# Layer 2 of a graph network: the input added by VectorE, a norm's statistics from sums on ScalarE, 28 single places for the diagonals

## The chip, the cores and the metric

The kernel runs on one core of one Trainium2 chip. The metric is the device time of one execution in microseconds. Instructions are told apart by engine: PE (TensorE's matmuls; PEld is its loading of weights), DVE (VectorE), ACT (ScalarE), POOL (GpSimd) and SP (SyncE). Each has its own queue and works it off in order; semaphores tie the queues together. POOL issues the indirect transfers and SP the plain ones, and both kinds share 16 DMA engines.

## The reference

A graph network of two attention layers over 10,000 nodes and 170,000 given edges, all in float32. Cut to what matters:

```python
def gat_conv(x, src, dst, W, a_src, a_dst, bias):     # self loops are added to the edges
    xl = x @ W                                        # per head
    e = leaky_relu((xl @ a_src)[src] + (xl @ a_dst)[dst], 0.2)
    alpha = softmax of e over the edges of one dst
    return segment_sum(xl[src] * alpha, dst) + bias

h1 = relu(layer_norm(gat_conv(x, W1 ...), g1, be1)) + (x @ Wr1 + br1)     # 4 heads x 256
h2 = layer_norm(gat_conv(h1, W2 ...), g2, be2) + (h1 @ Wr2 + br2)         # 1 head, 768
out = plain_layer_norm(x + h2)          # mean and variance over 768, no weights
```

The change lies in the last two lines: the weighted sum over a node's neighbours, its norm, the two additions and the plain norm behind them.

## The kernel before

**Tiles and slots.** The nodes are sorted by their number of edges into 79 tiles of 128, one node to a partition. A tile `t` has `SLOTS[t]` slots: slot k holds, for each of its 128 nodes, the row of the node's k-th neighbour in the table `h1 @ W2`, 768 numbers and 2 attention terms (394 KB a slot). There are 1371 slots in layer 2, 17.4 a tile on average; the list `turns` lets large and small tiles alternate, 25 and 12 slots at the start, 18 and 17 at the end. Layer 2 starts at about 3185 us.

**The ring.** A `Ring` of `RING2 = 41` slots in SBUF holds the rows. The first slot of a tile is the nodes' own rows, a plain transfer by SP (L501); the other 1292 are indirect gathers by POOL (L472). Slot q + 41 is fetched into the place of slot q behind the last use of slot q, in the order of the program, so POOL waits until PE and DVE have both read it.

**A tile's work.** `weights_of(t)` makes the softmax weights `e`: small DVE operations and an exponential on ACT (L543). The weighted sum is shared by columns. DVE multiplies and adds columns 0 to 511 of one slot after another into `acc` (L573). For columns 512 to 767, `summed` lets ACT make a diagonal matrix of each slot's weights (L1298: the identity, scaled by `e`), and PE multiplies it with the slot's 256 columns (L1299) into the second part of the PSUM tile `rs[t]`. The bias `b2` goes into that sum by the identity, too (`add_b2`, L1308). `residual(t)` fills the first part of `rs[t]`: x by the identity (L1350), and `h1 @ Wr2` in 8 blocks for each of two column ranges, 512 and 256 wide (L1353). Each float32 matmul shows as two records in the profile. The operands hT and xt of `residual` are loaded by SP (L1257, L1258) two tiles ahead, into pieces of the memory in which layer 1 kept `w2` (the name `w` in the profile, `w_88` in the listings, means such pieces: hT, xt and the sums `h`); the first two tiles' are loaded earlier, into `firsts`.

**The norms.** `norms(t)` runs during the loop over the slots of tile t + 1, in steps at its start and at slots k = 3, 6 and 9 (`LEAD = 3`): the statistics of the weighted sum (L584, L586 on DVE; the standard deviation by logarithm and exponential on ACT, L588 and L589); then the scaling (L598, L600), the addition of `rs[t]` (L1363) and the statistics of the second norm (L584, L586, L588, L589 again); then `less` on DVE (L1367) and the output on ACT (L1369); then the output's indirect scatter on POOL (L1371).

**What sets the order.** Each engine's order is that in which the program is written. The loop over tile t writes `residual(t + 1)` first, then its slots; at slot `turn` of it the logits of tile t + 1, at `turn + 3` the softmax's rest, `add_b2`, the diagonals and PE's products of tile t + 1. So PE's order is `residual(t + 1)`, products of t + 1, `residual(t + 2)`, and so on, and on ACT the diagonals of tile t + 1 stand ahead of the norm of tile t. The diagonals have 5 places for groups of `G = 4`: 20 diagonals.

Of the kernel before, what the change touches and what calls it, by code (L numbers as in the profile page):

```python
# [28 lines left out]
F32 = mybir.dt.float32  # L29
I32 = mybir.dt.int32  # L30
BF16 = mybir.dt.bfloat16
AF = mybir.ActivationFunctionType
OP = mybir.AluOpType
AX = mybir.AxisListType

P = 128
# [12 lines left out]
G = 4  # L49
RING1 = 31  # L50
RING2 = 41
LEAD = 3
DIAGONALS = 5
ON_PE2 = 512
SHARE = 4
ON_PE1 = 5
# [30 lines left out]
def gnn_kernel(ctx, tc, x, x_cols, src, dst, src_col, dst_col, W1, a_src1, a_dst1, b1, g1, be1, Wr1, br1,  # L87
               W2, a_src2, a_dst2, b2, g2, be2, Wr2, br2, out, n_edges):
    nc = tc.nc
    N, D0 = out.shape  # L90
    H1, DH1 = a_src1.shape
    H2, DH2 = a_src2.shape
    C1, C2 = H1 * DH1, H2 * DH2
# [3 lines left out]
    NT = -(-N // P)  # L97
# [19 lines left out]
    x_d = dram.tile([NT, P, D0], F32, name="x_d")  # L117
# [458 lines left out]
    def pieces(a, width):  # L576

        return [a[:, c:c + width] for c in range(0, a.shape[1], width)]

    def deviation(small, parts):  # L580

        st = small.tile([P, len(parts), 6], F32, name="st")
        for j, a in enumerate(parts):
            nc.vector.bn_stats(st[:, j, :], a)  # L584
        mv = small.tile([P, 2], F32, name="mv")
        nc.vector.bn_aggr(mv, st.rearrange("p k s -> p (k s)"))  # L586
        sd = small.tile([P, 1], F32, name="sd")
        nc.scalar.activation(sd, mv[:, 1:2], AF.Ln, bias=eps)  # L588
        nc.scalar.activation(sd, sd, AF.Exp, scale=-0.5)  # L589
        return mv[:, 0:1], sd  # L590
# [254 lines left out]
    def begin_layer2(mem):  # L845


        rest = mem.shape[1]

        def at_end(n):  # L850
            nonlocal rest
            rest -= n
            return mem[:, rest:rest + n]

        firsts = [(at_end(C1), at_end(D0)) for _ in range(min(2, NT))]
        for t, (hT, xt) in enumerate(firsts):
            nc.sync.dma_start(hT, h1_d[turns[t]])
            nc.sync.dma_start(xt, x_d[turns[t]])
        wr2 = wr1.rearrange("p k n -> p (k n)")[:, :K1 * C2].rearrange("p (k n) -> p k n", n=C2)
        load(wr2, Wr2)  # L860
        br, ones = at_end(C2), at_end(P)
        yield
        nc.vector.memset(ones, 1.0)
        nc.vector.tensor_scalar(br, wr2[:, 0, :], br1_c[:, 0:1], None, op0=OP.mult)
        for k in range(1, K1):
            nc.vector.scalar_tensor_tensor(br, wr2[:, k, :], br1_c[:, k:k + 1], br, op0=OP.mult, op1=OP.add)
        yield wr2, firsts, br, ones, rest
# [367 lines left out]
    def ordered_layer2(mem, begun):  # L1235
# [4 lines left out]
        with tc.tile_pool(name="b2", bufs=1) as pool, tc.tile_pool(name="small2", bufs=2) as small, \  # L1240
# [2 lines left out]

            wr2, firsts, br, sums_of, rest = begun
            parts = pieces(w2.rearrange("p k n -> p (k n)")[:, :6 * C1], C1)
            held = mem.shape[1] // R2
            tail = pool.tile([P, RING2 - held, R2], F32, name="ring")
            views = [mem[:, :held * R2].rearrange("p (k n) -> p k n", n=R2), tail]
            ring = Ring(table2, RING2, dict(zip(FIRST, (TURNS[t] for t in turns))), views, at)

            def fetch_x(t):

                if t < 2:
                    hT, xt = firsts[t]
                else:
                    hT, xt = parts[t % 2], parts[2 + t % 2][:, :D0]
                    nc.sync.dma_start(hT, h1_d[turns[t]])  # L1257
                    nc.sync.dma_start(xt, x_d[turns[t]])  # L1258
                return hT.rearrange("p (k n) -> p k n", n=P), xt

            ins = {0: fetch_x(0)}
            ring.fetch(SLOTS[0])
            adds = [spread(pool, shift, "out", nc.sync)]
            b2_b = spread(pool, b2, "b2", nc.sync)
            ins[1] = fetch_x(1)
            g2_b, be2_b = (spread_to(to[:, :C2], v, nc.sync) for to, v in zip(norm_b, (g2, be2)))
            nc.vector.tensor_add(b2_b, b2_b, adds[0][:, :C2])
            adds.append(spread(pool, br2, "out", nc.sync))
# [17 lines left out]
            def weights_of(t):  # L1286
# [6 lines left out]

                def summed(e, lo, hi, more=None, m=0):
                    for k in range(lo, hi):
                        if (k - lo) % G == 0:
                            diagonals = pool.tile([P, G, P], F32, name="diagonals", bufs=DIAGONALS)
                        nc.scalar.activation(diagonals[:, (k - lo) % G, :], ident, AF.Copy, scale=e[:, k - lo, :])  # L1298
                        nc.tensor.matmul(to, diagonals[:, (k - lo) % G, :], ring.slot(at + k)[:, ON_PE2:C2],  # L1299
                                         start=False, stop=(k == n - 1), skip_group_check=True)  # L1300
                        if k - lo < m:
                            nc.tensor.matmul(more, diagonals[:, (k - lo) % G, :], ring.slot(at + k)[:, :ON_PE2],
                                             start=False, stop=(k - lo == m - 1), skip_group_check=True)
                        if k - lo == m - 1:
                            nc.scalar.copy(ring.slot(at + lo)[:, :ON_PE2], more)
# [37 lines left out]
            def residual(t):  # L1343


                hT, xt = ins.pop(t)
                r = ps_big.tile([P, 2 * BANK], F32, name="big")
                for c in range(0, C2, BANK):
                    d = min(C2, c + BANK)
                    nc.tensor.matmul(r[:, c:d], ident, xt[:, c:d], start=True, stop=False,  # L1350
                                     skip_group_check=True)
                    for j in range(K1):
                        nc.tensor.matmul(r[:, c:d], hT[:, j, :], wr2[:, j, c:d], start=False,  # L1353
                                         stop=(j == K1 - 1 and d < C2),
                                         skip_group_check=True)
                return r

            def norms(t, h, r, means):

                stats = deviation(small, [a for m in means for a in pieces(m, C2 - ON_PE2)])  # L1360
                yield
                scaled(h, means, stats, g2_b, be2_b)
                nc.vector.tensor_add(h, h, r[:, :C2])  # L1363
                mean, inv = deviation(small, pieces(h, C2 // 2))
                yield
                less = small.tile([P, 1], F32, name="less")
                nc.vector.scalar_tensor_tensor(less, mean, -1.0, inv, op0=OP.mult, op1=OP.mult)  # L1367
                o = pool.tile([P, C2], F32, name="out")
                nc.scalar.activation(o, h, AF.Identity, bias=less, scale=inv)  # L1369
                yield  # L1370
                nc.gpsimd.indirect_dma_start(  # L1371
                    out=out, out_offset=bass.IndirectOffsetOnAxis(ap=nodes(turns[t]), axis=0),
                    in_=o, in_offset=None, bounds_check=N - 1, oob_is_err=False)
# [10 lines left out]
            for t in range(NT):  # L1384
# [19 lines left out]
                for k in range(n):  # L1404
# [15 lines left out]
                        if not lo or k - lo >= whole(t):  # L1420
                            weigh(acc, row, weights[:, k - lo], ON_PE2, None if k else b2_b)
                    ring.fetch(FIRST[t] + k + 1 + ring.size)
                    if t + 2 < NT and k == n // 2:
                        ins[t + 2] = fetch_x(t + 2)
                ready += itertools.islice(ahead, 2 - len(ready))
                for _ in last:
                    pass
# [1 line left out]
                    nc.vector.tensor_add(be2_b, be2_b, adds[1])  # L1429
                    nc.vector.tensor_add(be2_b, be2_b, q[:, :C2])  # L1430
                last = norms(t, h, rs[t], [acc, rs[t][:, C2:2 * C2 - ON_PE2]])
                if t + 2 < NT and t + 2 not in ins:
                    ins[t + 2] = fetch_x(t + 2)
            for _ in last:
                pass

# [270 lines left out]
```

## Time and profile before

| | |
|---|---|
| median of 3 runs | 5286.99 us (5283.68 to 5294.54) |
| the profiled execution | 5287.85 us, span 5286.1 us, mean granted TensorE clock 0.943 |
| PE busy | 4742.8 us (90%), 14012 records |
| DVE busy | 4326.7 us (82%) |
| POOL busy | 3432.3 us (65%) |
| ACT busy | 3084.4 us (58%) |
| moved by DMA | 1588 MB, mean 300 GB/s |

The shares are means over the whole span. Layer 2 is the last 2.1 ms of it and has a mix of its own, so it is read by windows that lie within it. In rows of groups, what stands before the bar is the busy time and the mean time of one instruction in ns; behind it is the idle time of the engine just before such instructions, with what ended most of it. "issue" there is time in which the engine waited for nothing that the profile shows. In rows of a timeline, the first number is the start, the second the duration, and the bracket holds the idle time before it and what ended it.

### The profile page before, as it was taken

The page shows a single profiled execution, that of the slowest core. Times are in us where ns is not written, and L with a number is a line of the kernel's source. Part 1 is how long each engine was busy: PE and PEld are TensorE (multiplying, and loading weights), DVE is VectorE, ACT ScalarE, POOL GpSimd, SP SyncE. Part 2 cuts the span into 40 slices and gives each one's busy share as a digit, 9 for nine tenths or more (in the row PEclk, how much of TensorE's full clock was granted, in tenths as well). Part 3 has the DMA queues.
Part 4 walks back from the last instruction along what each step waited for, and adds up shares of the span by engine and source line. Part 5 has one row for each costly group of instructions (what it writes and reads, how often), then busy time and mean ns, then how long its engine had stood idle before and what let it go on. Part 6 is the DMA issues. An engine that isn't in the chain of part 4 may idle for free. (4 is left out here: it accounts for less than half of the span.)

```text
span 5286.1 us, 57927 instructions
## 1 busy us (share of the span) xinstructions
PE 4742.8 (90%) x14012; PEld 2650.4 (50%) x14012; DVE 4326.7 (82%) x7168; ACT 3084.4 (58%) x8710; POOL 3432.3 (65%) x3722
## 2 busy tenths in 40 slices
PE   9999998999999979899999997888888887888886
PEld 4444444554444434444445554555555555555554
DVE  7887877998998988889999975877878777777776
ACT  5744446899999988898999862322222322222222
POOL 6867756666777766677766626666666666666664
PEclk9999998999999989999999998889898898888888
DMA  4423459999999989999999959988899898888885
GB/s 153 131 94 129 112 174 338 350 365 367 382 387 395 376 299 339 344 372 380 376 373 370 349 199 328 327 316 313 313 320 315 310 320 305 305 299 301 303 302 191
DMA packets 433439, 1588.37 MB, mean 300 GB/s; under 512 B 77207, under 2 KB 82135, under 8 KB 433094
## 3 DMA queue, kind: packets, MB, share of 16 engines
q0 software_dynamic: 321040, 1283.72, 67.4%
q1 hardware_dynamic: 99490, 269.38, 14.1%
q10 hardware_dynamic: 12564, 31.47, 1.8%
q8 instruction: 118, 1.93, 0.1%
q14 instruction: 227, 1.86, 0.1%
HBM read 1426.26 MB, written 177.29 MB: 303 GB/s over the span
## 5 line engine op out<-in xcount | busy, mean ns | idle before, releaser
L472 POOL DMA_INDIRECT ring<-table,slots x2663 | 2636.4, 990 | 1490.6 <-issue 569.8
L562 ACT ACTIVATE ring<-ring,e 128x256 f32<-128x256 f32 x4468 | 1823.6, 502 | 65.7 <-DVE e L981 34.3
L573 DVE SCALAR_TENSOR_TENSOR acc<-ring,e,acc 128x512 f32<-128x512 f32 (+1 forms) x2280 | 1454.0, 638 | 104.2 <-PE acc L936 27.1
L569 DVE TENSOR_TENSOR acc<-acc,ring 128x1024 f32<-128x1024 f32 x869 | 1070.2, 1231 | 80.7 <-ACT ring L562 16.9
L1353 PE MATMUL big<-wr,w 128*128 128x512 f32 (+1 forms) x2464 | 877.3, 501 | 148.9 <-issue 147.4
L1299 PE MATMUL big<-ring,diagonals 128*128 128x256 f32 x2742 | 723.9, 419 | 182.6 <-issue 166.2
L1161 PE MATMUL half<-w,hT 128*128 128x512 f32 (+1 forms) x2528 | 844.0, 486 | 5.5 <-issue 5.2
L179 PE MATMUL big<-wr,xT 128*128 128x512 f32 x1896 | 836.4, 598 | 0.3 <-ACT xT L897 0.3
L1299 PEld LDWEIGHTS big<-ring,diagonals 128*128 128x128 f32 x2742 | 582.4, 213 | 323.4 <-issue 220.1
L1298 ACT ACTIVATE diagonals<-ident,e 128x128 f32<-128x128 f32 x1371 | 419.6, 388 | 546.9 <-PE big L1299 215.8
L1353 PEld LDWEIGHTS big<-wr,w 128*128 128x128 f32 x2464 | 480.6, 196 | 511.8 <-issue 482.7
L1161 PEld LDWEIGHTS half<-w,hT 128*128 128x128 f32 x2528 | 472.6, 189 | 349.7 <-issue 310.4
L179 PEld LDWEIGHTS big<-wr,xT 128*128 128x128 f32 x1896 | 358.0, 192 | 422.3 <-issue 421.6
L936 PE MATMUL acc<-ring,ident 128*128 128x512 f32 x992 | 469.5, 622 | 76.6 <-ACT ring L562 49.3
L588 ACT ACTIVATE sd<-mv,eps 128x1 f32<-128x1 f32 x237 | 69.3, 292 | 683.7 <-issue 261.1
L936 PEld LDWEIGHTS acc<-ring,ident 128*128 128x128 f32 x992 | 191.3, 198 | 317.0 <-issue 193.2
L694 ACT ACTIVATE scr<-scr 128x256 f32<-128x256 f32 x624 | 250.5, 403 | 160.7 <-DVE scr L687 155.6
L634 PE MATMUL one<-wr,mixed 128*128 128x512 f32 x702 | 307.6, 592 | 0.0
L699 POOL TENSOR_TENSOR row<-row,none 128x1024 f32<-128x1024 f32 x69 | 168.1, 2437 | 117.2 <-DVE scr L687 45.8
L634 PE MATMUL one<-w,xT 128*128 128x512 f32 x492 | 228.6, 602 | 7.7 <-DMA w<-in_W_dram 5.4
L584 DVE BATCH_NORM_STATS2 st<-big 128x6 f32<-128x256 f32 x79 | 33.4, 423 | 242.3 <-remote 122.8
L634 PEld LDWEIGHTS one<-wr,mixed 128*128 128x128 f32 x702 | 133.4, 190 | 167.9 <-issue 167.2
(239 smaller groups left out, 4334.0 us busy)
## 6 DMA issues: line engine op xcount, KB each, us to landing
ring<-table,slots POOLq DMA_INDIRECT x2663
h_d<-hT SPq DMA_DIRECT2D x79, 512.0 KB
table<-row SPq DMA_DIRECT2D x78, 516.0 KB
w<-h_d SPq DMA_DIRECT2D x77, 512.0 KB
table<-row SPq DMA_DIRECT2D x79, 385.0 KB
ring<-table SPq DMA_DIRECT2D x79, 385.0 KB
x_d<-xt SPq DMA_DIRECT2D x77, 384.0 KB
w<-x_d SPq DMA_DIRECT2D x77, 384.0 KB
```

What stands on the lines that cost most here:

```text
L179: nc.tensor.matmul(p[:, c:e], aT[:, j, :], w[:, j, c:e], start=(j == 0), stop=(j == k - 1))
L472: nc.gpsimd.indirect_dma_start(out=to, out_offset=None, in_=table, in_offset=bass.IndirectOffsetOnAxis(ap=index, axis=0), **more)
L562: nc.scalar.activation(row[:, s], row[:, s], AF.Copy, scale=e[:, h:h + 1])
L569: nc.vector.tensor_add(acc[:, :c], acc[:, :c], row[:, :c])
L573: nc.vector.scalar_tensor_tensor(acc[:, s], row[:, s], e[:, h:h + 1], (acc if first is None else first)[:, s], op0=OP.mult, op1=OP.add)
L634: nc.tensor.matmul(p, aT[:, j, :], w[:, j, :], start=(start and j == 0), stop=(j == k - 1), skip_group_check=True)
L694: nc.scalar.activation(m[:, s], m[:, s], AF.Copy, accum_out=row[:, C1 + i * H1 + h:C1 + i * H1 + h + 1])
L936: nc.tensor.matmul(acc[:, c:c + BANK], ident, ring.slot(q + k)[:, c:c + BANK], start=(k == 0), stop=(k == m - 1))
L1161: nc.tensor.matmul(q, hT[:, j, :], w2[:, j, c:c + q.shape[1]], start=(j == 0), stop=(j == K1 - 1))
L1298: nc.scalar.activation(diagonals[:, (k - lo) % G, :], ident, AF.Copy, scale=e[:, k - lo, :])
L1299: nc.tensor.matmul(to, diagonals[:, (k - lo) % G, :], ring.slot(at + k)[:, ON_PE2:C2], start=False, stop=(k == n - 1), skip_group_check=True)
L1353: nc.tensor.matmul(r[:, c:d], hT[:, j, :], wr2[:, j, c:d], start=False, stop=(j == K1 - 1 and d < C2), skip_group_check=True)
```

## The change

1. **x.** PE's product of the identity and x (L1350) goes. VectorE adds x to `h` in `norms(t)`, behind the addition of `rs[t]`. The loads are parted: `fetch_h` still loads hT two tiles ahead, `fetch_x` loads x one tile ahead, at the same point of the loop, into the same two pieces of `w`. That load now waits for VectorE's addition of the tile before the last, where it had waited for PE's reading.
2. **The second norm.** VectorE's statistics of it and `less` go. ScalarE makes them in two passes over the 768 columns that also sum up: a copy for the sum, then, with the negative mean as bias, a square for the variance; then logarithm, exponential and a product for the output's scale and bias.
3. **The diagonals.** 28 single places take the place of 5 groups of 4, 20 in a tile of their own and 8 in the ends of pieces of `w` that are 1024 columns long and hold 768. They are taken in turn.

```diff
-DIAGONALS = 5
+DIAGONALS = 20
...
+            diagonals = pieces(pool.tile([P, DIAGONALS * P], F32, name="diagonals"), P)
+            for part in parts[2:]:
+                diagonals += pieces(part[:, C1 - 2 * P:], P)
+            turning = itertools.cycle(diagonals)
...
+            def fetch_h(t):
+                if t < 2:
+                    hT = firsts[t]
+                else:
+                    hT = parts[t % 2]
+                    nc.sync.dma_start(hT, h1_d[turns[t]])
+                return hT.rearrange("p (k n) -> p k n", n=P)
             def fetch_x(t):
-                if t < 2:
-                    hT, xt = firsts[t]
-                else:
-                    hT, xt = parts[t % 2], parts[2 + t % 2][:, :D0]
-                    nc.sync.dma_start(hT, h1_d[turns[t]])
-                    nc.sync.dma_start(xt, x_d[turns[t]])
-                return hT.rearrange("p (k n) -> p k n", n=P), xt
+                xt = parts[2 + t % 2][:, :D0]
+                nc.sync.dma_start(xt, x_d[turns[t]])
+                return xt
...
                 def summed(e, lo, hi, more=None, m=0):
                     for k in range(lo, hi):
-                        if (k - lo) % G == 0:
-                            diagonals = pool.tile([P, G, P], F32, name="diagonals", bufs=DIAGONALS)
-                        nc.scalar.activation(diagonals[:, (k - lo) % G, :], ident, AF.Copy, scale=e[:, k - lo, :])
+                        diagonal = next(turning)
+                        nc.scalar.activation(diagonal, ident, AF.Copy, scale=e[:, k - lo, :])
...
             def residual(t):
-                hT, xt = ins.pop(t)
+                hT = ins.pop(t)
...
-                    nc.tensor.matmul(r[:, c:d], ident, xt[:, c:d], start=True, stop=False,
-                                     skip_group_check=True)
...
                 nc.vector.tensor_add(h, h, r[:, :C2])
-                mean, inv = deviation(small, pieces(h, C2 // 2))
+                nc.vector.tensor_add(h, h, xs.pop(t))
                 yield
-                less = small.tile([P, 1], F32, name="less")
-                nc.vector.scalar_tensor_tensor(less, mean, -1.0, inv, op0=OP.mult, op1=OP.mult)
                 o = pool.tile([P, C2], F32, name="out")
+                less, inv = (small.tile([P, 1], F32, name=n) for n in ("less", "inv"))
+                nc.scalar.activation(o, h, AF.Copy, accum_out=less)
+                nc.scalar.activation(less, less, AF.Copy, scale=-1.0 / C2)
+                nc.scalar.activation(o, h, AF.Square, bias=less, accum_out=inv)
+                nc.scalar.activation(inv, inv, AF.Ln, scale=1.0 / C2, bias=eps)
+                nc.scalar.activation(inv, inv, AF.Exp, scale=-0.5)
+                nc.scalar.activation(less, less, AF.Copy, scale=inv)
                 nc.scalar.activation(o, h, AF.Identity, bias=less, scale=inv)
...
-                    if t + 2 < NT and k == n // 2:
-                        ins[t + 2] = fetch_x(t + 2)
+                    if k == n // 2:
+                        if t + 2 < NT:
+                            ins[t + 2] = fetch_h(t + 2)
+                        if t + 1 < NT:
+                            xs[t + 1] = fetch_x(t + 1)
```

In the listings of the two programs, PE's queue where one tile's products end and the next tile's residual begins, before (`big` is `rs[t]`, `w_88` here xt in L1350's rows and hT in L1353's, `wr_89` Wr2, the semaphores in brackets are what a row waits for):

```order
L1299 MATMUL big<-ring,diagonals 128x256 [waits DMASW7_49,Activation_49]
L1350 MATMUL big<-w_88,ident 128x512 [waits DMAHW5_49,DVE_49,PE_49]
L1353 MATMUL big<-wr_89,w_88 128x512 [waits DMAHW4_49]
L1353 MATMUL big<-wr_89,w_88 128x512 x7
L1350 MATMUL big<-w_88,ident 128x256
L1353 MATMUL big<-wr_89,w_88 128x256 x8
L1308 MATMUL big<-b_22697,ident 128x256
L1299 MATMUL big<-ring,diagonals 128x256 [waits DMAHW2_49,Activation_49]
```

The same place after:

```order
L1306 MATMUL big<-ring,diagonals 128x256 [waits DMASW3_49,Activation_49]
L1358 MATMUL big<-wr_89,w_88 128x512 [waits DMAHW7_49,DVE_49,PE_49]
L1358 MATMUL big<-wr_89,w_88 128x512 x7
L1358 MATMUL big<-wr_89,w_88 128x256 x8
L1315 MATMUL big<-b_22696,ident 128x256
L1306 MATMUL big<-ring,diagonals 128x256 [waits DMAHW6_49,Activation_49]
```

Two matmuls are gone from each tile, and with them the wait for x's transfer; the rest stands as it did.

ACT's queue at a tile of 24 slots, before: the end of its diagonals, then the first norm's standard deviation of the tile before it (L588, L589, the first pair), the second norm's (the second pair), the output, and the exponential of the next tile:

```order
L1298 ACTIVATE diagonals<-ident,e 128x128 [waits PE_49]
L1298 ACTIVATE diagonals<-ident,e 128x128 x3
L588 ACTIVATE sd<-mv,eps 128x1 [waits DVE_49]
L589 ACTIVATE sd<-sd 128x1 [waits Activation_49]
L588 ACTIVATE sd<-mv,eps 128x1 [waits DVE_49]
L589 ACTIVATE sd<-sd 128x1 [waits Activation_49]
L1369 ACTIVATE out<-w_88,less,sd 128x768 [waits DMASW0_49,DVE_49]
L543 ACTIVATE e<-e 128x13 [waits DVE_49]
```

The same place after (`inv` is first the sum of squares, then the scale; `less` first the sum, then the bias):

```order
L1305 ACTIVATE diagonals<-ident,e 128x128 [waits PE_49] x16
L1305 ACTIVATE w_88<-ident,e 128x128 [waits PE_49] x7
L588 ACTIVATE sd<-mv,eps 128x1 [waits DVE_49]
L589 ACTIVATE sd<-sd 128x1 [waits Activation_49]
L1373 ACTIVATE out,less<-w_88 128x768 [waits DMASW0_49,DVE_49]
L1374 ACTIVATE less<-less 128x1 [waits Activation_49]
L1375 ACTIVATE out,inv<-w_88,less 128x768 [waits Activation_49]
L1376 ACTIVATE inv<-inv,eps 128x1 [waits Activation_49]
L1377 ACTIVATE inv<-inv 128x1 [waits Activation_49]
L1378 ACTIVATE less<-less,inv 128x1 [waits Activation_49]
L1379 ACTIVATE out<-w_88,less,inv 128x768 [waits Activation_49]
L543 ACTIVATE e<-e 128x13 [waits DVE_49]
```

Every diagonal now has a wait of its own for PE's reading of its place, 28 diagonals back, where the first of each group of four had one. Between the first norm's standard deviation and the next exponential, three instructions have become seven, with two more passes over 768 columns among them; only the first of the seven waits for VectorE.

## What I predict, and why

> **What bounds the kernel now.** I read the slices of the page first, then the windows of layer 2, its groups by form, the waits, and single tiles on the timeline. The chain that ended last is no help: it breaks off after the last output scatter. The slices:
>
> ```profile
> PEclk9999998999999989999999998889898898888888
> DMA  4423459999999989999999959988899898888885
> ...
> POOL out_dram L1371 0%; POOLq L1654 0%
> ```
>
> The change touches layer 2 alone, the last 2.1 of 5.3 ms (slices 24 to 40). Its steady part as one window (columns: window, its length, PE, PEld, DVE, ACT and POOL busy with their instructions, granted TensorE clock, DMA share, GB/s):
>
> ```profile
> 3240.00:5230.00 1990.00, 1660.76 (x5464) 1119.59 (x5465) 1511.75 (x3019) 565.72 (x1773) 1266.49 (x1314) 0.89 0.89 310
> ```
>
> No engine is full: PE 83%, the DMAs 89%, DVE 76%, POOL 64%, ACT 28%. Four short stretches inside it, with the same columns, show why:
>
> ```profile
> 3328.00:3360.00 32.00, 32.00 (x114) 21.26 (x113) 30.41 (x69) 11.59 (x37) 22.68 (x23) 1.00 0.98 362
> 4168.00:4185.00 17.00, 17.00 (x62) 11.36 (x60) 9.33 (x15) 4.78 (x15) 12.87 (x14) 1.00 0.96 344
> 4185.00:4195.00 10.00, 2.51 (x6) 1.42 (x6) 7.89 (x14) 0.99 (x4) 5.21 (x6) 0.70 0.89 325
> 4195.00:4198.00 3.00, 2.84 (x7) 2.27 (x7) 2.79 (x9) 0.74 (x2) 0.28 (x1) 0.50 0.43 86
> ```
>
> In the last three, one tile runs in a cycle. PE goes at full rate for 17 us with the DMAs nearly full; then for 10 us it gets only six matmul records out, while the DMAs go on; then the DMAs fall to 0.43, PE works again at half clock, and the cycle starts over. What PE waits for in such a stretch is in the groups (busy us, mean ns | idle before it, and what ended that):
>
> ```profile
> L1299 PE MATMUL big<-ring,diagonals 128*128 128x256 f32 x2606 | 690.8, 421 | 169.8 <-issue 154.4 <-DMA ring<-table,slots 7.4 <-ACT out L1369 2.4
> L1353 PE MATMUL big<-wr,w 128*128 128x512 f32 x1210 | 540.7, 599 | 4.1 <-issue 4.0
> L1353 PE MATMUL big<-wr,w 128*128 128x256 f32 x1200 | 317.4, 401 | 137.9 <-issue 136.5
> ```
>
> Of PE's 329 idle us (1990 less 1661), these rows put 295 down to "issue", no wait that the profile shows, and about 17 to anybody else. So PE never waits for diagonals, for x or for DVE: it is the engine that is late, and the others wait for it. The gathers too:
>
> ```profile
> POOL ring L472 <- PE big L1299: 226.1, 133, 7.5
> ...
> POOL ring L472 <- DVE acc L573: 47.3, 79, 5.5
> ...
> POOL ring L472 <- DVE w L600: 8.9, 5, 4.0
> ```
>
> A ring slot comes free when PE (columns 512 on) and DVE (columns up to 512) are through with it; POOL waits 226 us for PE there. The floor under this is the DMAs: 1990 us at 310 GB/s are 617 MB, and at the 362 GB/s of the first short window, where the tiles are small and PE is never idle, they would take 1704 us, 286 us less.
>
> **The change, part by part.** The x product goes from PE. Four records a tile, and the time to the next record after each pair (start, us, operation):
>
> ```profile
> 3628.46 1.02 PE L1350 MATMUL big<-w,ident 128*128 128x512 f32 x2
> 3629.31 7.03 PE L1353 MATMUL big<-wr,w 128*128 128x512 f32 x16
> 3636.18 0.59 PE L1350 MATMUL big<-w,ident 128*128 128x256 f32 x2
> 3636.61 3.62 PE L1353 MATMUL big<-wr,w 128*128 128x256 f32 x16
> ```
>
> 0.85 + 0.43 = 1.28 us a tile, 79 tiles: 101 us at full clock, 114 at the granted 0.89. If PE sets the pace alone, all 114 come off. If the DMAs do, nothing: PE then only reaches its slow stretch earlier. The rows put it between. The DMAs need a fixed part of each cycle, and only the part in which they are quiet can shrink: 0.98 less 0.89 of 1990 us is 179 us, 2.4 us a tile, room for the 1.28. But that part also holds the first gathers' way back, which the change leaves alone. I take half, **-57 us**, and keep 0 and -114.
>
> The diagonals: five groups of four make 20 places today, a tile with more slots takes them again, and then ACT waits for PE to begin the same tile, with the norm of the tile before behind it in its queue:
>
> ```profile
> 3512.80 1.27 ACT L1298 ACTIVATE diagonals<-ident,e 128x128 f32<-128x128 f32 x4 [8.10 <-PE big L1299]
> ...
> 3514.53 1.02 DVE L600 SCALAR_TENSOR_TENSOR w<-w,sd,norm 128x768 f32<-128x768 f32 x1 [9.78 <-ACT sd L589]
> ```
>
> The diagonals came 8.10 us late, the standard deviation behind them too, and DVE waited 9.78 us for it. Over the steady part, that line's group:
>
> ```profile
> L600 DVE SCALAR_TENSOR_TENSOR w<-w,sd,norm 128x768 f32<-128x768 f32 x75 | 76.5, 1020 | 130.2 <-ACT sd L589 85.1 <-ACT sd L588 27.2 <-ACT diagonals L1298 11.4
> ```
>
> With 28 places a tile of up to 28 slots never waits for itself, so DVE's 124 us at L600 go. They are worth 124 at most and 0 at least: when they end, DVE waits instead for the late PE at its next statistics, as it does where tiles have 20 slots or fewer (235.5 us, below). What reaches the gathers is the row of POOL's waits that L600 ended, 8.9 us: **-9 us**.
>
> The second norm and the addition, DVE's side and ACT's:
>
> ```profile
> L584 DVE BATCH_NORM_STATS2 st<-big 128x6 f32<-128x256 f32 x75 | 31.7, 423 | 235.5 <-remote 122.8 <-PE big L1353 59.5 <-issue 42.6
> ...
> L584 DVE BATCH_NORM_STATS2 st<-w 128x6 f32<-128x384 f32 x150 | 76.5, 552 | 2.6
> ...
> L586 DVE BATCH_NORM_AGGREGATE mv<-st 128x2 f32<-128x12 f32 x75 | 15.7, 209 | 2.6
> ...
> L1367 DVE SCALAR_TENSOR_TENSOR less<-mv,sd 128x1 f32<-128x1 f32 x76 | 11.6, 152 | 0.0
> ...
> L1363 DVE TENSOR_TENSOR w<-w,big 128x768 f32<-128x768 f32 x75 | 71.5, 953 | 2.6
> ...
> L1369 ACT ACTIVATE out<-w,less,sd 128x768 f32<-128x768 f32 x76 | 77.4, 1018 | 56.9 <-DVE less L1367 30.0 <-DVE acc L573 16.2 <-issue 7.4
> ...
> L588 ACT ACTIVATE sd<-mv,eps 128x1 f32<-128x1 f32 x150 | 43.8, 292 | 635.8 <-issue 252.4 <-DVE mv L586 230.6 <-DVE st L584 152.5
> ```
>
> DVE loses 76.5 + 15.7 + 11.6 = 104 us and gains 75 additions of 0.95, 71 us: 33 us less, on an engine that waits 235.5 us for PE anyway. 0, between 0 and -33. ACT gains, a tile, two passes over 128x768 (each 1.02 at most, the row with two pointers) and two one-column scalings (0.29 at most); logarithm and exponential are there before too. At most 2.6 us a tile, 207 us over 79 tiles, on an engine idle for 1990 - 566 = 1424 us. Its cover is twofold. The next tile's diagonals stand behind the chain, but PE waits for ACT only in the 2.4 us of the L1299 row above. And the output scatter stands behind it in POOL's queue, ahead of gathers:
>
> ```profile
> 3520.13 1.03 ACT L1369 ACTIVATE out<-w,less,sd 128x768 f32<-128x768 f32 x1 [1.73 <-DVE less L1367]
> ...
> 3526.70 1.02 POOL L1371 DMA_INDIRECT out_dram<-out,order  x1 [0.30 <-ACT diagonals L1298]
> ```
>
> The result lies ready 5.5 us before POOL comes to it; 2.6 fit. If both covers were gone it would cost the 207. 0. The Trainium skill speaks against this move: "ScalarE: Activation LUTs", section "Rules for kernel authors", gives additions and multiplications to VectorE, since ScalarE is slower at them. By that rule the swap would lose the difference of the two engines' times; no run so far shows such a loss here, since ACT is idle 72% of the part.
>
> The loads: x now comes a tile later, behind the same h load on SP, and waits for DVE's addition of the tile before last; it is read more than a tile after. The bytes are the same. 0, within a microsecond either way. At the end nothing hides the last norm:
>
> ```profile
> 5270.67 0.95 DVE L1363 TENSOR_TENSOR w<-w,big 128x768 f32<-128x768 f32 x1
> 5271.66 1.02 DVE L584 BATCH_NORM_STATS2 st<-w 128x6 f32<-128x384 f32 x2
> ...
> 5272.96 0.29 ACT L588 ACTIVATE sd<-mv,eps 128x1 f32<-128x1 f32 x1 [4.06 <-DVE mv L586]
> 5273.28 0.20 ACT L589 ACTIVATE sd<-sd 128x1 f32<-128x1 f32 x1
> ...
> 5273.71 1.03 ACT L1369 ACTIVATE out<-w,less,sd 128x768 f32<-128x768 f32 x1 [0.23 <-DVE less L1367]
> ```
>
> From 5271.66 to 5273.71 are 2.05 us today. After: 0.95 for the second addition, then on ACT 1.02 for the sum, 0.29 for the mean, 1.02 for the squares, 0.29 + 0.20 for logarithm and exponential, 0.29 for the last scaling: 4.06, so **+2 us**.
>
> Sum: the profiled execution took 5287.85 us (0.9 above the median of the three); 5287.85 - 57 - 9 + 2 = 5224.
>
> **Rivals.** *All of PE's time comes through.* For it: PE waits for nobody, and small tiles ran at 362 GB/s with PE 100% busy. Against: the average tile is larger. 5287.85 - 114 - 9 + 2 = 5167; with part of DVE's 124 beside it, down to about 5135.
>
> *The DMAs keep the pace.* PE's freed time turns into idle time, and idle time lowers its clock, as at 4195 (0.50 after ten us with a quarter busy). For it: the slow stretch ends only as the DMAs go quiet. Against: they are quiet 9% of the time. 5287.85 + 2, less up to 9: 5281 to 5290, no change. The Trainium skill has this clock rule in "TensorE: Matmul & The Clock Gate", section "Why this matters for your kernels": about 3 us without matmuls bring the clock back to half. The trace's 0.50 agrees.
>
> *Slower: the slow stretches lengthen.* Place: 4185 to 4195, once a tile. If slots come free earlier, POOL finds more of them, the DMAs don't go quiet, and PE stays in the stretch for each further gather; at 325 GB/s one of 394 KB is 1.21 us. One more a tile is 96 us over 79, two are 191. It decides from (57 + 9 - 2) / 79 = 0.81 us a tile on. With one and a half, 5224 + 144 = 5368; with one, 5320. Against it: at 3328 the DMAs stayed at 0.98 for 32 us and PE lost nothing.
>
> **How the numbers follow.** About 0.2% (11 us) is what a measurement here tells from no change. My forecast, a part of the cut passed on (5198 to 5258, -90 to -30): 0.42. All passed on (5135 to 5198): 0.18. A remnant only (5258 to 5276): 0.11. No change: 0.16. Slower: 0.13. Faster is 0.42 + 0.18 + 0.11 = 0.71. The range leaves out the slower case and a little on the fast side: 5150 to 5294.
>
> **What would show it.** Right: the additions of x on DVE at 0.95 us, PE's busy time in layer 2 lower by about 100 us, no waits of 8 us or more on ACT's standard deviations, the DMA share of the steady part at 0.91 to 0.92, and still one slow stretch a tile. All passed on: a share of 0.94 or more, 328 GB/s. The DMAs pace: the share stays at 0.89 and the clock or the "issue" idle takes what L1350 leaves. Slower: the "issue" idle of L1299 and the residual's line grows by over 60 us. Wrong altogether: POOL waiting for ACT at the scatter, or PE for diagonals, by more than 30 us.

## The result, and the profile after

The changed kernel takes 5228.1 us (median of 6 runs, 5219.95 to 5242.6) against 5286.13 us for the kernel before (6 runs): a ratio of 0.9895, 95% interval 0.9877 to 0.9913, 58 us less. That pair was measured on a chip on which PE has the late stretches that the prediction describes. The experiments below fell on three other chips, where PE has none and the kernel before takes 4930 us. On the one of them where the whole change was run, it makes the kernel **slower**, by a ratio of 1.008 (1.0067 to 1.0094). (No number is known of the first chip; that it is none of these three is taken from the 357 us between the times of the same kernel.) Both results are told here, since the second could not be guessed from the first.

The profiled execution after took 5226.69 us. Its slices (the clock that the throttle granted, and the DMA share, in tenths), with layer 2 from slice 25 on:

```profile
PEclk9999998999999998999999998888888988888898
DMA  4323449999999989999999968998999999998995
```

Towards the end of layer 2 the DMA row now reads 9 where it read 8. The same part of layer 2 as a window, 60 us shorter than before, with the columns of the prediction's windows:

```profile
3240.00:5170.00 1930.00, 1577.83 (x5205) 1068.57 (x5205) 1502.23 (x2808) 739.66 (x2243) 1313.55 (x1315) 0.88 0.91 320
```

PE is busy 83 us less than the 1660.76 of before, and its idle time grew from 329 to 352 us. The DMAs went from 0.89 to 0.91 and from 310 to 320 GB/s. What PE waits for:

```profile
PE big L1306 <- issue: 201.6, 152, 3.1
PE big L1358 <- issue: 78.6, 64, 2.9
PE big L1315 <- issue: 31.9, 21, 3.6
PE big L1306 <- DMA ring<-table,slots: 15.6, 12, 2.4
```

The three "issue" rows sum to 312 us. Before, they were 154.4, 140.5 (4.0 and 136.5 in the prediction's groups) and 17.3, 312 as well. So PE's late time is all still there, with 8 PE records fewer in a tile (four matmuls and four weight loads). What shrank is the time in which the DMAs are quiet: the DMAs' unused time in the two windows, their length less the DMAs' busy share of it, was 223 us before and is 174 us now, 49 of the 60 us.

The gathers on POOL, before and then after, over the same two windows:

```profile
L472 POOL DMA_INDIRECT ring<-table,slots x1237 | 1188.0, 960 | 700.4 <-issue 248.1 <-PE big L1299 226.1 <-remote 70.8
```

```profile
L472 POOL DMA_INDIRECT ring<-table,slots x1239 | 1233.8, 996 | 591.2 <-issue 248.0 <-PE big L1306 149.0 <-remote 73.3
```

POOL's pauses before gathers shrank by 109 us, 77 of them its wait for PE. But the gathers themselves took 46 us longer, which the prediction has nothing for.

On VectorE and ScalarE (busy us, mean ns | idle before, and what ended it), over that window:

```profile
L1373 ACT ACTIVATE out<-w 128x768 f32<-128x768 f32 x76 | 63.2, 832 | 126.5 <-DVE w L1369 43.4 <-issue 31.9 <-DMA out_dram<-out,order 29.6
...
L600 DVE SCALAR_TENSOR_TENSOR w<-w,sd,norm 128x768 f32<-128x768 f32 x76 | 77.4, 1018 | 46.2 <-ACT sd L589 28.3 <-issue 4.9 <-remote 3.6
L1369 DVE TENSOR_TENSOR w<-w 128x768 f32<-128x768 f32 x76 | 72.8, 958 | 3.0 <-DVE w L1368 0.5
...
L1375 ACT ACTIVATE out<-w,less 128x768 f32<-128x768 f32 x76 | 71.1, 935 | 2.5
...
L584 DVE BATCH_NORM_STATS2 st<-big 128x6 f32<-128x256 f32 x75 | 31.9, 426 | 258.6 <-remote 164.7 <-PE big L1358 66.7 <-issue 18.9
```

VectorE's 130 us at L600 fell by 84 to 46, and the longest wait for a standard deviation there is 6.7 us. Its wait at the first statistics, where the prediction expected the time again, rose from 235.5 to 258.6, by 23: a part of the stall was handed on, in a window that is itself 60 us shorter. The end of the program, from the last statistics to the output:

```profile
5204.57 0.42 DVE L584 BATCH_NORM_STATS2 st<-big 128x6 f32<-128x256 f32 x1
...
5208.58 0.96 DVE L1369 TENSOR_TENSOR w<-w 128x768 f32<-128x768 f32 x1
5209.57 0.84 ACT L1373 ACTIVATE out<-w 128x768 f32<-128x768 f32 x1 [3.75 <-DVE w L1369]
...
5212.73 1.03 ACT L1379 ACTIVATE out<-w,less,inv 128x768 f32<-128x768 f32 x1
```

From the addition of x to the output's start are 4.15 us, where the prediction counted 4.06.

### The profile page after: what moved, and what is told of

It is laid out like the page before. It is cut to its first block, busy times and chain, and to the rows that moved or that the text cites. A ratio compares the mean times of both kernels' runs of the same rounds, so it can differ in the third digit from the quotient of the medians.

```text
span 5224.9 us, 57558 instructions
## 1 busy us (share of the span) xinstructions
PE 4638.3 (89%) x13696; PEld 2586.3 (49%) x13696; DVE 4306.4 (82%) x6931; ACT 3261.5 (62%) x9184; POOL 3485.8 (67%) x3722
## 5 line engine op out<-in xcount | busy, mean ns | idle before, releaser
L472 POOL DMA_INDIRECT ring<-table,slots x2663 | 2682.5, 1007 | 1370.1 <-issue 543.9
L573 DVE SCALAR_TENSOR_TENSOR acc<-ring,e,acc 128x512 f32<-128x512 f32 (+1 forms) x2280 | 1457.5, 639 | 98.7 <-PE acc L935 21.2
L1358 PE MATMUL big<-wr,w 128*128 128x512 f32 (+1 forms) x2464 | 842.8, 495 | 85.1 <-issue 83.8
L1306 PE MATMUL big<-ring,diagonals 128*128 128x256 f32 x1960 | 545.5, 427 | 193.0 <-issue 147.9
L1306 PEld LDWEIGHTS big<-ring,diagonals 128*128 128x128 f32 x1960 | 421.8, 217 | 309.7 <-issue 208.0
L543 ACT ACTIVATE e<-e 128x19 f32<-128x19 f32 (+14 forms) x82 | 17.6, 215 | 537.8 <-DVE e L542 167.5
L1305 ACT ACTIVATE diagonals<-ident,e 128x128 f32<-128x128 f32 x980 | 296.5, 387 | 79.3 <-DVE e L553 37.0
L588 ACT ACTIVATE sd<-mv,eps 128x1 f32<-128x1 f32 x158 | 46.1, 292 | 463.2 <-DVE mv L586 245.6
L1306 PE MATMUL big<-ring,w 128*128 128x256 f32 x782 | 224.2, 430 | 68.4 <-issue 58.2
```

The costliest lines, as they stand in the source:

```text
L472: nc.gpsimd.indirect_dma_start(out=to, out_offset=None, in_=table, in_offset=bass.IndirectOffsetOnAxis(ap=index, axis=0), **more)
L573: nc.vector.scalar_tensor_tensor(acc[:, s], row[:, s], e[:, h:h + 1], (acc if first is None else first)[:, s], op0=OP.mult, op1=OP.add)
L1305: nc.scalar.activation(diagonal, ident, AF.Copy, scale=e[:, k - lo, :])
L1306: nc.tensor.matmul(to, diagonal, ring.slot(at + k)[:, ON_PE2:C2], start=False, stop=(k == n - 1), skip_group_check=True)
```

## The experiments

The twelve kernels fell on three chips, four on each, and each four are compared with the kernel before on the same chip: 4931.3 us for the first four, 4930.0 for the second and 4931.2 for the third. The times in the first four expectations are those of the first chip (5287 us before), so there only the ratio can be compared.

**One part at a time.** *x alone* undoes the other two parts of the change:

```diff
-                        diagonal = next(turning)
+                        if (k - lo) % G == 0:
+                            diagonals = pool.tile([P, G, P], F32, name="diagonals", bufs=DIAGONALS)
...
+                mean, inv = deviation(small, pieces(h, C2 // 2))
```

> The kernel before with the first part alone: VectorE adds x, PE's product by the identity is gone, x is loaded a tile later. The second norm and the 20 places in groups are as before. My theory (the time of PE's cut passes through by about half): 57 us less and 1 us more at the end, 5230, between 5215 and 5250. Rival 'the places gave the gain' or 'the norm gave it': 5276 to 5290. Rival 'all of PE's 114 us passes and another part gives 57 back': 5170 to 5185.

Measured: 4973.61 us, ratio 1.0082 (1.0068 to 1.0096), 42 us more. None of the three theories had it slower.

*The places alone* is the kernel before with 28 single places:

```diff
-DIAGONALS = 5
+DIAGONALS = 20
...
+                        diagonal = next(turning)
+                        nc.scalar.activation(diagonal, ident, AF.Copy, scale=e[:, k - lo, :])
```

> The kernel before with the third part alone: 28 single places for the diagonals. My theory: VectorE's 124 us of waiting at L600 become waiting for PE, 9 us less: 5277, between 5268 and 5290. Rival 'the places gave the gain': 5250 or less. A third outcome, slower than 5296: each diagonal's own wait costs.

Measured: 4932.67 us, 1.0002 (0.9993 to 1.0011): nothing.

*The norm alone* is the kernel before with ScalarE's sums:

```diff
-                mean, inv = deviation(small, pieces(h, C2 // 2))
...
+                nc.scalar.activation(o, h, AF.Copy, accum_out=less)
+                nc.scalar.activation(less, less, AF.Copy, scale=-1.0 / C2)
+                nc.scalar.activation(o, h, AF.Square, bias=less, accum_out=inv)
```

> The kernel before with the second part alone: ScalarE makes the second norm's mean and variance from sums. My theory: 104 us less on VectorE and some 200 us more on ScalarE are both covered, 5286 with 1 us more at the end, between 5276 and 5296. Rival 'VectorE's relief gave the gain': 5240 to 5265. Rival 'ScalarE's slower passes cost': with 20 places in groups ScalarE's queue is late in the first half of layer 2, and the longer chain stands behind it, 5300 or more.

Measured: 4929.64 us, 0.9997 (0.9988 to 1.0006): nothing.

*x back on PE* has the norm and the places changed, and `residual` with its product by the identity as before:

```diff
+                    nc.tensor.matmul(r[:, c:d], ident, xt[:, c:d], start=True, stop=False,
+                                     skip_group_check=True)
...
-                nc.vector.tensor_add(h, h, xs.pop(t))
```

> The second and third part together, x by PE as before. My theory: 9 us less for the places, 1 us more at the end, 5278, between 5265 and 5290. Rival 'all of PE's 114 us passes, and these two parts cost 57': 5330 to 5345. Rival 'the two give the gain': 5225 to 5245.

Measured: 4930.11 us, 0.9999 (0.999 to 1.0008). On this chip the whole effect is in x, and it is a loss. How the chip differs is in the rows of *x back* (PE's waits between 3200 and 4800 us, all that are over 10 us; then that window):

```profile
PE big L1303 <- ACT diagonals L1302: 74.9, 24, 6.3
PE big L1303 <- ACT w L1302: 30.6, 10, 5.9
PE big L1303 <- DMA ring<-table,slots: 11.6, 4, 3.7
```

```profile
3200.00:4800.00 1600.00, 1470.35 (x5224) 1025.30 (x5222) 1343.76 (x2581) 694.95 (x2108) 1204.96 (x1248) 0.96 0.98 367
```

No "issue" is left: PE is in time, has 130 us to spare and waits for ScalarE now and then, and the DMAs hardly go quiet (0.98, 367 GB/s). PE is not the engine that is late here.

**The whole change on such a chip, and parts of it undone.** *The changed kernel again*, with no edit:

> The changed kernel itself. The last four runs fell on a chip on which the kernel before takes 4931 us and PE has no stretches of late records; the prediction was made for one with such stretches (5287). If the DMAs keep the pace on such a chip (their share was 0.98 to 0.99 of 3200 to 4800 us there): 4920 to 4945, no change. If PE's time still counts there: 4870 to 4890. If VectorE counts, as the 4974 of 'x alone' suggests, the second norm's move makes up for it: again 4920 to 4945. If this run falls on a chip with the stretches: 1.1% under the kernel before, as measured.

Measured: 4970.61 us, 1.008 (1.0067 to 1.0094). None of the three cases fits: it is 41 us slower.

*The places back*: the changed kernel with groups of four.

```diff
-                        diagonal = next(turning)
+                        if (k - lo) % G == 0:
+                            diagonals = pool.tile([P, G, P], F32, name="diagonals", bufs=DIAGONALS)
```

> The changed kernel with the 20 places in groups of four instead of the 28 single ones (x and the norm stay changed). My theory: the places are worth 9 us at most, so within 0.3% of the changed kernel. Rival 'without the places ScalarE's longer queue is late': 1% or more above the changed kernel, with PE waiting for diagonals.

Measured: 4972.01 us, 1.0081 (1.0067 to 1.0095), as the changed kernel.

*The norm back*: the changed kernel with the second norm's statistics on VectorE.

```diff
+                mean, inv = deviation(small, pieces(h, C2 // 2))
...
-                nc.scalar.activation(o, h, AF.Copy, accum_out=less)
```

> The changed kernel with the second norm on VectorE again (x by VectorE and the 28 places stay). Where PE has no late stretches: VectorE has 0.95 us a tile more than before and nothing less, as in 'x alone', 4965 to 4980. Rival 'it was the places that x alone lacked': 4920 to 4945. Where PE has the stretches: VectorE waits for PE anyway, within 0.3% of the changed kernel.

Measured: 4970.26 us, 1.0083 (1.007 to 1.0097). The number is the expected one and its reason falls: this kernel gives VectorE 85 us more between 3200 and 4800 us than the changed one (1469 against 1384 us busy) and takes the same time. VectorE's load is not what costs 40 us.

*More instructions on PE at the same work*:

```diff
-                for c in range(0, C2, BANK):
+                for c in range(0, C2, BANK // 2):
```

> The changed kernel with h1 @ Wr2 in column ranges of 256, 256 and 256 instead of 512 and 256: PE's busy time is the same (0.43 us for two records of 256 columns, 0.85 for two of 512), but a tile has 32 more instructions on PE, 188 instead of 156. If the late stretches are a matter of time alone, or there are none: within 0.3% of the changed kernel. Rival 'while the DMAs are full, PE gets its instructions late, about 0.7 us for each': 5 us a tile or more where the stretches are, 400 us and more; where the DMAs are full all the time and there are no stretches, still no change.

Measured: 4969.22 us, 1.0074 (1.006 to 1.0088), as the changed kernel. With PE on time, 32 more instructions a tile cost nothing; whether they do in the late stretches isn't answered, since no run of it fell on a chip that has them.

What does cost 40 us shows on POOL. In the changed kernel on the chip without stretches, VectorE's norm and the gathers beside it, from one timeline:

```profile
4029.98 1.02 DVE L600 SCALAR_TENSOR_TENSOR w<-w,sd,norm 128x768 f32<-128x768 f32 x1
4030.28 1.53 POOL L472 DMA_INDIRECT ring<-table,slots  x1 [0.30 <-issue]
4031.03 0.95 DVE L1368 TENSOR_TENSOR w<-w,big 128x768 f32<-128x768 f32 x1
4032.02 0.96 DVE L1369 TENSOR_TENSOR w<-w 128x768 f32<-128x768 f32 x1
4032.12 1.67 POOL L472 DMA_INDIRECT ring<-table,slots  x1 [0.30 <-DVE w L1368]
4032.90 2.33 DVE L573 SCALAR_TENSOR_TENSOR acc<-ring,e,acc 128x512 f32<-128x512 f32 x3
4034.10 0.95 POOL L472 DMA_INDIRECT ring<-table,slots  x1 [0.30 <-issue]
```

A gather takes 0.95 us to issue and the next follows after 0.30. The gather that starts at 4032.12, just after the addition of x began, takes 1.67 us, which is the 0.86 us left of the addition and some 0.8 of its own. The one that starts inside L600 (4030.28) is late in the same way. Those two operations read two tensors from SBUF; L1368 reads one from SBUF and one from PSUM. The group of gathers between 3200 and 4800 us, in *x back* and then in the changed kernel:

```profile
L472 POOL DMA_INDIRECT ring<-table,slots x1176 | 1132.4, 963 | 372.7 <-issue 90.1 <-PE big L1303 76.8 <-DVE acc L573 54.9
```

```profile
L472 POOL DMA_INDIRECT ring<-table,slots x1151 | 1150.7, 1000 | 355.8 <-issue 88.1 <-PE big L1306 72.8 <-DVE acc L573 46.7
```

The pause before a gather is 0.317 and 0.309 us in the mean, hardly more than the 0.30 that is always there. With the output's scatters and their pauses (97 and 94 us), POOL's queue is taken up for the whole 1600 us in both kernels: it issues without a stop, and 25 gathers fewer in the same time in the changed one. 37 ns more a gather over 1292 gathers are 48 us, against 41 measured. Counted one by one, 32 gathers in that window take over 1.1 us in *x back* and 106 in the changed kernel. Since the DMAs are nearly full as well (0.98 and 0.97), these rows alone do not say which of the two sets the pace. The next four kernels, which change only additions of VectorE, do.

**Where x is added.** *x into PSUM*: the same two additions, with the sum of x made in the PSUM tile.

```diff
-                nc.vector.tensor_add(h, h, r[:, :C2])
-                nc.vector.tensor_add(h, h, xs.pop(t))
+                nc.vector.tensor_add(r[:, :C2], r[:, :C2], xs.pop(t))
+                nc.vector.tensor_add(h, h, r[:, :C2])
```

> The changed kernel, with VectorE's addition of x made into the PSUM tile (r = r + x, then h = h + r): the same two additions by length, but none with both inputs in SBUF. In the changed kernel on the chips with PE on time, a gather that runs beside the addition of x takes 1.46 us on POOL instead of 0.95, and POOL issues gathers without a pause. Theory 'the two inputs in SBUF hold up POOL's gathers': the 40 us that the changed kernel loses there come back, 4920 to 4940 (before: 4930), with about 30 long gathers instead of 106 between 3200 and 4800 us. Rival 'the shorter PE or x's later load costs it': 4960 to 4975. On a chip with the late stretches: 5200 to 5228, since the lock costs there too.

Measured: 4928.41 us, 0.9992 (0.9983 to 1.0001); 44 long gathers (over 1.1 us). The 40 us are back. The same place of its timeline:

```profile
4032.39 1.02 DVE L600 SCALAR_TENSOR_TENSOR w<-w,sd,norm 128x768 f32<-128x768 f32 x1
4032.62 1.62 POOL L472 DMA_INDIRECT ring<-table,slots  x1 [0.30 <-PE big L1306]
4033.32 0.96 DVE L1368 TENSOR_TENSOR big<-big,w 128x768 f32<-128x768 f32 x1
4034.32 0.95 DVE L1369 TENSOR_TENSOR w<-w,big 128x768 f32<-128x768 f32 x1
4034.55 0.95 POOL L472 DMA_INDIRECT ring<-table,slots  x1 [0.30 <-DVE big L1368]
```

The gather that starts 0.23 us into the second addition takes 0.95 us. It is so all through that window: in the changed kernel 69 gathers start during the addition of x, 68 of them are long, and the mean is 1.55 us; in *x into PSUM* 68 start during the second addition, and none takes more than 0.97.

*x by another operation*, both inputs in SBUF:

```diff
-                nc.vector.tensor_add(h, h, xs.pop(t))
+                nc.vector.scalar_tensor_tensor(h, h, 1.0, xs.pop(t), op0=OP.mult, op1=OP.add)
```

> The changed kernel, with x added by scalar_tensor_tensor (h * 1.0 + x) instead of tensor_tensor. Both inputs still lie in SBUF. If any VectorE operation with two inputs in SBUF holds up the gathers: as the changed kernel, 4960 to 4980. If it is this operation's form alone (L600 is such a scalar_tensor_tensor, and the gathers beside it take 1.05 to 1.1 us in the mean): 4925 to 4945. On a chip with the late stretches: within 0.5% of the changed kernel.

Measured: 4968.46 us, 1.0072 (1.0058 to 1.0086); 106 long gathers. It is where the inputs lie, not the operation. The rest of VectorE's work agrees. Its multiply-adds (L573) read one slot from SBUF and `acc` from PSUM, and none of the 613 gathers that start during them in the changed kernel is long; only a tile's first multiply-add reads `b2` from SBUF in the place of `acc`, and there 18 of 35 are.

*x left out* (x is still loaded, and is missing from the output):

```diff
-                nc.vector.tensor_add(h, h, xs.pop(t))
+                xs.pop(t)
```

> The changed kernel without the addition of x (x is loaded and left out of the output): PE's cut alone, with nothing on VectorE for it. Theory of the hold-up: 4915 to 4935 where PE is on time, no gain from PE's 101 us, since POOL's gathers pace it. Rival 'the cut itself or the later load costs': 4955 to 4975. On a chip with the late stretches, my prediction's theory: 5190 to 5228.

Measured: 4931.37 us, 1.0 (0.9991 to 1.0009). PE's cut alone is worth nothing on such a chip, and neither it nor the later load costs anything.

*One more addition in the kernel before*:

```diff
                 nc.vector.tensor_add(h, h, r[:, :C2])
+                nc.vector.tensor_add(h, h, g2_b)
```

> The kernel before with one more addition a tile on VectorE, h + g2, both in SBUF, behind the addition of the residual (the output is changed by it); PE and all loads as before. Theory of the hold-up: 30 to 50 us more than the kernel before, 4960 to 4980, with some 100 long gathers. Rival 'VectorE has 76 us to spare and the addition is hidden': 4925 to 4937. On a chip with the late stretches: 0 to 40 more.

Measured: 4975.1 us, 1.0089 (1.0075 to 1.0103); 102 long gathers. PE and the loads are as before, and one addition of two SBUF tensors a tile makes a loss of the same size, 44 us:

```profile
4028.51 0.96 DVE L1364 TENSOR_TENSOR w<-w,norm 128x768 f32<-128x768 f32 x1
4028.61 1.68 POOL L472 DMA_INDIRECT ring<-table,slots  x1 [0.30 <-DVE w L1363]
4030.59 0.95 POOL L472 DMA_INDIRECT ring<-table,slots  x1 [0.31 <-DVE st L584]
```

## Why the prediction was right, and what it missed

- **The bound** held on the chip whose profile was shown: PE late in stretches, the DMAs quiet behind them. The predicted signs came: PE's busy time from 3185 us on 1724 to 1628 us ("lower by about 100"), a DMA share of 0.91, additions of 0.958 us, no wait of 8 us or more for a standard deviation, one slow stretch in most tiles. (Counted as two or more gaps of over 0.15 us in PE's stream, less than 1 us apart, there are 66 before and 61 after, 397 and 427 us in all.) All this is read from traces: no part of the change was tried alone on that chip.
- **-57 for PE's 114** was half by choice between two ends, and that the total came out at -58 is in part luck. The traces fit its mechanism: the time came from the quiet part of the DMAs (49 of 60 us), and PE's late time stayed. But the -58 is what is left of two sizes that the sum does not have, POOL's pauses shorter by 109 us and its gathers longer by 46. How much of the 109 is PE's cut and how much the places, and what the 46 cost there, is not shown. It did not foresee where the time comes from either. By windows of 260 us, the first and the last two (before, then after):

```profile
3240.00:3500.00 260.00, 218.46 (x726) 144.90 (x727) 203.56 (x415) 76.25 (x240) 170.11 (x175) 0.88 0.91 319
...
4540.00:4800.00 260.00, 220.12 (x705) 147.34 (x705) 192.41 (x386) 72.06 (x226) 161.47 (x169) 0.89 0.88 303
4800.00:5060.00 260.00, 213.44 (x688) 144.86 (x687) 194.01 (x389) 73.60 (x226) 157.43 (x165) 0.88 0.87 299
```

```profile
3240.00:3500.00 260.00, 215.34 (x707) 144.84 (x707) 202.11 (x382) 101.16 (x303) 172.60 (x174) 0.86 0.91 316
...
4540.00:4800.00 260.00, 210.68 (x682) 143.16 (x682) 199.30 (x374) 99.57 (x302) 174.41 (x178) 0.87 0.90 320
4800.00:5060.00 260.00, 214.95 (x719) 148.18 (x718) 210.50 (x395) 103.52 (x316) 175.73 (x178) 0.90 0.92 322
```

  The transfer rate is about the same at the start of layer 2 (319 and 316 GB/s) and 17 to 23 GB/s higher towards its end. Why the early part, where the tiles' sizes differ most, gains little stays open.
- **-9 for the places** was too much: *the places alone* and *the places back* show nothing either way (1.0002; 4972.0 against 4970.6 us), on chips where ScalarE's diagonals never wait long for PE (with groups of four, 3.0 us at most between 3200 and 4800 us in *one more addition*). On the first chip they were not tried alone; the row that the 9 stood for, POOL's waits that L600 ended, fell there from 8.9 to 5.4 us.
- **0 for the second norm** was right where it was tried alone: 0.9997. The added work is 0.832 + 0.187 us for the sum, 0.935 + 0.187 for the squares (each pass has a short read of its sum behind it), and 0.203 + 0.294 for the scalings, 2.64 us a tile against the "at most 2.6" estimated; the second pass with its read takes 1.12 us where the prediction had 1.02 at most. The Trainium skill's rule that speaks against the move ("ScalarE: Activation LUTs", section "Rules for kernel authors") agrees by the instruction and not by the kernel: ScalarE's two passes take 2.14 us, VectorE's statistics and `less` took 1.46, and the kernel's time is the same.
- **+2 at the end** was right: from the start of the last statistics of PSUM to that of the output's scatter, 7.37 us before (5267.65 to 5275.02) and 9.46 after (5204.57 to 5214.03), 2.09 more.
- **0 to -33 for VectorE's addition is the step that failed.** It counted VectorE's own time and the wait for PE that covers it. It did not ask what the operation holds: POOL's gathers. That costs POOL 0.6 us a tile in the mean (58 us above 0.95 in the long gathers of 70 tiles, 15 us in *x back*). On the first chip it is in the trace too (30 gathers over 1.1 us between 3200 and 4800 us before, 88 after), and the gathers took 46 us longer. POOL still waits 149 us for PE there, so a part of it may be covered; how much is not shown. On the other chips POOL has no slack, and 0.6 us over 79 tiles, 48 us, are the whole result of 41. The prediction's "slower" rival had another cause, so its price, 5320 to 5368, answers to nothing that was seen.
- **The clock at 4195.** The prediction sets its 0.50 beside the Trainium skill's figure of about 3 us without matmuls ("TensorE: Matmul & The Clock Gate", section "Why this matters for your kernels"). The half agrees and the gap does not: PE's longest gap between 4185 and 4195 us is 2.23 us, and it ran a record every one to three us. Nothing in the sum hangs on it.
- The Trainium skill states what was missed: "SBUF — State Buffer", section "SBUF: two separate sides", says that VectorE and GpSimd share one pair of ports, that an operation of VectorE with two inputs in SBUF takes it as an exclusive lock against a GpSimd operation that reads SBUF, and that the later one waits until it is over. The traces agree for a gather that comes second: up to 1.68 us instead of 0.95 beside two SBUF inputs, 0.95 beside one input in SBUF and one in PSUM. Its words that a lock is held "for the whole instruction" are seen as well on VectorE's side: the later into the addition a gather starts, the less it is held up (1.65 us for those that start 0.1 to 0.2 us into it, 1.27 for 0.5 to 0.6). They are not seen on GpSimd's side: of the 70 additions of x in that window, the 18 that start while POOL is issuing an indirect transfer take 0.96 us and start 0.03 us after the operation before them, as the other 52 do.

Left open: why PE is late on one chip and not on three others, or whether it is the chip at all. The kernel before, unchanged, takes 5287 us on the one and 4930 on the others; 32 more PE instructions a tile change nothing where there are no stretches; and none of the twelve kernels fell on a chip that has them. So which part of the change gave the 58 us there is not shown by a run. *x into PSUM* loses nothing where PE is on time; whether it keeps the gain, or adds to it, where PE is late was not measured.

## What to carry to other kernels

Before moving work to an engine, ask what it locks as well as how long it takes: an indirect transfer whose issue starts while VectorE reads two SBUF tensors is held up until VectorE is through (up to 1.68 us instead of 0.95 here), and an operand in PSUM avoids that at the same length (0.95 us an addition). Look at the pause between the issues of a queue: here it was a steady 0.30 us, and the queue set the pace though its engine shows as 75% busy, so that the hold-ups were paid nearly in full. And a stall that the profile calls "issue", with nothing named that ended it, may not be there on the next chip: a change that pays by shortening what goes with it can lose there.

## What the runs showed of the hardware

- The same kernel takes 5287 us on one chip and 4930 to 4931 on three others; from the first tile's logits in layer 2 to the last's are 2055 us on the one and 1745 on another (read from *x back*, which takes as long as the kernel before there), and the one has PE's late stretches in that part, 397 us in 66 of them. The other 48 us lie ahead of layer 2 and were not looked into.
- A gather's issue that starts during a VectorE operation with two SBUF inputs takes up to 1.7 us instead of 0.95: it ends some 0.8 us after the operation. It is so whether the operation is an addition or a scalar_tensor_tensor; one such addition a tile costs 37 to 44 us of 4930.
- PE's granted clock between 3200 and 4800 us is 0.96 in *x back* and 0.93 in *x left out*, where PE is busy for 1397 instead of 1470 us; the time is the same.
